# Storing the sampling hats of a deformable convolution with columns and rows apart, and loading the row hats of both halves at once

## The chip, the cores and the metric

The kernel runs on one core of one Trainium2 chip. A core has a matrix engine (PE), a vector engine (DVE), an activation engine (ACT), a general engine (POOL) and a queue processor (SP) that here only issues transfers. Each engine takes its instructions in order, and they meet through semaphores. Transfers are issued from three queues (SP, ACT and POOL) and are carried by 16 DMA engines that all queues share. The metric is the device time of one execution in microseconds (us), lower is better. Three runs of the kernel before took 9085.48, 9095.87 and 9104.18 us; the median is 9095.87 us.

## The reference

Two layers are computed on 32 images of 96 channels and 56 x 56 pixels, in float32.

The first is a squeeze-and-excite block: a 1x1 convolution to 576 hidden channels, a depthwise 3x3 convolution, a gate per channel from the mean of each hidden channel, a 1x1 convolution back to 96 channels, and the residual. Its result is called x1.

The second takes spectra of x1 by two-dimensional Fourier transforms, makes a channel gate `ca` and a pixel gate `sa` from them, and forms y = x1 * ca * sa. From y it computes 18 offsets per pixel (nine taps, two coordinates), a gate and an ordinary 3x3 convolution. Then comes the deformable convolution:

```python
px = xx + off[:, :, 0]
py = yy + off[:, :, 1]
sampled = _grid_sample_taps(y, px, py)      # bilinear: four neighbours, four weights
y_def = jnp.einsum('bcthw,oct->bohw', sampled, def_w.reshape(c, c, 9)) + def_b
z = (1 - gate) * y_base + gate * y_def
```

z is normalised over the batch, x1 is added, and a ReLU follows. Bilinear sampling at px weighs column i with max(0, 1 - |i - px|), and likewise for rows. That function is the "hat" of this text: the weight of a pixel is its column hat times its row hat.

## The kernel before

**Tiles of the sampling.** An image is cut into 7 bands of 8 rows. A band holds 14 tile columns (`NTX`) of 4 pixels, and each has two tiles of 4 x 4 pixels, an upper (s = 0) and a lower one (s = 1). A tile samples from the 8 x 8 pixels around it (`SB` = 8, `NS` = 64). For a tile the weights are a matrix of 64 source pixels by 9 taps x 16 pixels (`KP` = 144). Upper and lower tile lie on partitions 0 to 63 and 64 to 127, so that a weight tile has 128 partitions. A band is worked in two halves h of 7 tile columns (`NTH`), so that a row of a weight tile holds 7 x 144 = 1008 numbers, which is 4032 bytes.

**How the hats are made.** `offsets` (lines 651 to 688) copies the offsets of a band from PSUM (L661), stores them to DRAM as `od` (L665, POOL queue), and loads them back eight times over as `ht` (L677, SP queue): 112 partitions, one for each of 8 positions i and 14 tile columns t, and in the free dimension four pieces of 144 numbers in the order column hats of s = 0, row hats of s = 0, column hats of s = 1, row hats of s = 1. Its inner function `hats` takes |ht + blk| and then relu(1 - ...) in place (L682 and L683, both on ACT), and stores the result as `hd[x][i][t][n]` (L685, ACT queue), x being the piece of the four.

**How they are loaded.** `weights_load` (L691) fills two tiles of 128 x 1008 for one half of a band by four transfers on SP's queue. For s = 0 and for s = 1, `wc` takes column hats (L698) with the eight rows i repeated as a block, and `wr` takes row hats (L699) with each row i repeated eight times. Each transfer fills 64 partitions. The source pattern of L698 is 8 (step 0) x 8 x 1008, that of L699 is 8 x 8 (step 0) x 1008. `weights` multiplies the two tiles on DVE (L705), and the result feeds the sampling matmuls of `sample_tiles` (L734), 28 for each half. The pool of `wc` has three buffers and that of `wr` two. All pools have a buffer set for each tile name.

**What runs beside it.** While the bands of image b are sampled, image b + 1 goes through `attend` (the projection at L329 from `hq` tiles that SP loads at L311, then the Fourier transforms, whose inputs SP loads at L369 into the same `hq` tiles, the matmuls L393 and the sums L379), and image b + 2 goes through `hidden` (matmuls L169, depthwise taps on DVE at L262). `pump` steps these two streams. The half bands give a natural count: 14 of them make one image, and one image takes about 265 us. The projection begins at the start of an image's 14 half bands, and the first transform comes two half bands later.

**What sets the order.** Instructions of PE, DVE, ACT and POOL are put in order by a scheduler that works with its own estimates of durations. SP's queue is left out of that and keeps the order of the program text: a transfer that waits holds up all transfers behind it. The tile `hq` has one buffer for each of its two names.

Of the kernel before, what the change touches and what calls it, by code (L numbers as in the profile page):

```python
# [7 lines left out]
FP = mybir.dt.float32  # L8
I32 = mybir.dt.int32
AF = mybir.ActivationFunctionType  # L10
# [27 lines left out]
NTX = W // TS  # L38
NTH = NTX // 2
# [3 lines left out]
SB = TS + 2 * REACH  # L43
NS = SB * SB
KP = NTAP * TP
# [580 lines left out]
def joint_conv(nc, p, yp, j, hid):  # L626


    w = p["w"]
    pa = bank(p)  # L630
    conv3(nc, pa[:, :BW], w["joint"], yp, CJ, j)
    nc.scalar.activation(hid, pa[:DMID, :BW], AF.Relu, bias=w["dg1b"][:DMID])  # L632
    yb = p["yb"].tile([C, BW], FP, name="yb")
    yield yb, pa[OFF0 : OFF0 + NOFF, :BW]
    nc.scalar.activation(yb[BC:], pa[OFF0 + QC :, :BW], AF.Identity, bias=w["cv"]("base_b")[BC:])
    pb = bank(p)
    for k in range(NTAP):
        dy, dx = divmod(k, 3)
        r0 = j * RB + dy + PD - 1
        for i in range(2):  # L640
            nc.tensor.matmul(pb[i * BC : (i + 1) * BC, : BW // 2].rearrange("p (h w) -> p h w", h=RB // 2), w["base"][:, k],  # L641
                             yp[:C, r0 + i * RB // 2 : r0 + (i + 1) * RB // 2, dx + PD - 1 : dx + PD - 1 + W],
                             start=(k == 0), stop=(k == NTAP - 1))
    yield
    for i in range(2):
        nc.scalar.activation(yb[:BC, i * BW // 2 : (i + 1) * BW // 2], pb[i * BC : (i + 1) * BC, : BW // 2], AF.Identity,
                             bias=w["cv"]("base_b")[:BC])
    yield


def offsets(nc, p, yp, j, top, hid, ybs, hds, defer):

    w = p["w"]
    joint = joint_conv(nc, p, yp, j, hid)
    yb, pa = next(joint)
    ybs.append(yb)
    at = p["off"].tile([NOFF, NTX, 2, TP], FP, name="at")
    for s in range(2):  # L660
        nc.vector.tensor_copy(at[:, :, s].rearrange("o t (r c) -> o t r c", r=TS),  # L661
                              pa[:, s * BW // 2 : (s + 1) * BW // 2].rearrange("o (r t c) -> o t r c", r=TS, t=NTX))
    yield
    od = p["dp"].tile([NTX, 2, NOFF, TP], FP, name="od")
    nc.gpsimd.dma_start(od.rearrange("t s o p -> o (t s) p"), at.rearrange("o t s p -> o (t s) p"))  # L665
    yield
    next(joint)
    yield
    next(joint)
    yield  # L670
    next(joint, None)
    nc.vector.tensor_reduce(top, at.rearrange("o t s p -> o (t s p)"), AX.X, ALU.max, apply_absolute_value=True)
    for _ in range(4):
        yield
    ht = p["ht"].tile([SB * NTX, 4, KP], FP, name="ht")
    src = od.rearrange("t s o p -> t (s o p)").unsqueeze(0).to_broadcast([SB, NTX, 4 * KP])
    nc.sync.dma_start(ht.rearrange("q n k -> q (n k)"), src)  # L677
    for _ in range(6):
        yield

    def hats():
        p["tc"].keep_in_program_order(nc.scalar.activation(ht, ht, AF.Abs, bias=w["blk"]))  # L682
        nc.scalar.activation(ht, ht, AF.Relu, bias=w["one"], scale=-1.0)  # L683
        hd = p["dp"].tile([4, SB, NTX, KP], FP, name="hd")
        nc.scalar.dma_start(hd.rearrange("x i t n -> (i t) x n"), ht)  # L685
        hds.append(hd)

    defer(hats)


def weights_load(nc, p, hd, h):  # L691

    src = hd.rearrange("n i t k -> n i (t k)")[:, :, h * NTH * KP : (h + 1) * NTH * KP]
    wc = p["wc"].tile([2 * NS, NTH * KP], FP, name="wc")
    wr = p["wr"].tile([2 * NS, NTH * KP], FP, name="wr")
    for s in range(2):
        ps = slice(s * NS, (s + 1) * NS)
        nc.sync.dma_start(wc[ps], src[2 * s].unsqueeze(0).to_broadcast([SB, SB, NTH * KP]))  # L698
        nc.sync.dma_start(wr[ps], src[2 * s + 1].unsqueeze(1).to_broadcast([SB, SB, NTH * KP]))  # L699
    return wc, wr  # L700


# [246 lines left out]
def layers(tc, a, dp, x1d, zd, stats, far):  # L949
# [8 lines left out]
    with ExitStack() as ctx:  # L958
# [144 lines left out]
        def prepare(upto):  # L1103

            nonlocal n_loads
            while n_loads < min(upto, 2 * len(hds)):
                n, m = divmod(n_loads, 2)
                loads.append(weights_load(nc, p, hds[n], m))
                n_loads += 1
# [402 lines left out]
```

## Time and profile before

| | before |
|---|---|
| median of three runs | 9095.87 us |
| profiled execution | 9085.91 us |
| its span, first to last instruction | 9084.1 us |
| PE busy | 8142.0 us (90%) |
| DVE busy | 7141.8 us (79%) |
| ACT busy | 5374.6 us (59%) |
| POOL busy | 2782.8 us (31%) |
| granted PE clock, mean | 0.943 |
| DMA moved | 1486.53 MB, 164 GB/s |
| `wc` transfers (L698) | 896 of 252 KB |
| `wr` transfers (L699) | 896 of 252 KB |

The profile is of one execution, so a sum made on it is made against 9085.91 us, which lies 9.96 us under the median. In the span's 40 slices PE is busy nine tenths or more from the fourth to the thirty-seventh. The end is different: from 8800 to 9084 us PE does nothing, and the normalisation moves data at 407 GB/s. In a view of waits a line names the instruction that waited, its engine, and what released it, then the total in us, the number of waits and the longest. In a view of windows the columns are the stretch, its length, the busy time of five engines with their counts of instructions, the granted clock (1.00 is full), the mean busy share of the 16 DMA engines, and GB/s.

### The profile page before, as it was taken

The page shows a single profiled execution, that of the slowest core. Times are in us where ns is not written, and L with a number is a line of the kernel's source. Part 1 is how long each engine was busy: PE and PEld are TensorE (multiplying, and loading weights), DVE is VectorE, ACT ScalarE, POOL GpSimd, SP SyncE. Part 2 cuts the span into 40 slices and gives each one's busy share as a digit, 9 for nine tenths or more (in the row PEclk, how much of TensorE's full clock was granted, in tenths as well). Part 3 has the DMA queues.
Part 4 walks back from the last instruction along what each step waited for, and adds up shares of the span by engine and source line. Part 5 has one row for each costly group of instructions (what it writes and reads, how often), then busy time and mean ns, then how long its engine had stood idle before and what let it go on. Part 6 is the DMA issues. An engine that isn't in the chain of part 4 may idle for free. (4 is left out here: it accounts for less than half of the span.)

```text
span 9084.1 us, 138191 instructions
## 1 busy us (share of the span) xinstructions
PE 8142.0 (90%) x52406; PEld 5146.5 (57%) x52406; DVE 7141.8 (79%) x6821; ACT 5374.6 (59%) x10486; POOL 2782.8 (31%) x2608
## 2 busy tenths in 40 slices
PE   5889999999999999999999999999999999999860
PEld 3455565565555566555655655565565555566640
DVE  7688788888878788888888888788888888887333
ACT  2356666666656566666666666665666666666553
POOL 0123233333323333332333333233333323333210
PEclk9889999999999999999999999999999999999985
DMA  2355555555555555555555555555655555555559
GB/s 84 104 142 164 162 167 163 165 152 153 166 163 167 163 166 152 154 163 164 167 165 163 156 153 163 162 168 164 166 153 152 165 163 164 167 166 146 127 183 417
DMA packets 1068763, 1486.53 MB, mean 164 GB/s; under 512 B 590190, under 2 KB 839838, under 8 KB 1055806
## 3 DMA queue, kind: packets, MB, share of 16 engines
q1 hardware_dynamic: 858995, 985.20, 39.8%
q10 hardware_dynamic: 153803, 329.80, 10.0%
q0 software_dynamic: 55296, 162.60, 7.0%
q8 instruction: 421, 6.90, 0.3%
q14 instruction: 248, 2.03, 0.1%
HBM read 1064.29 MB, written 412.65 MB: 163 GB/s over the span
## 5 line engine op out<-in xcount | busy, mean ns | idle before, releaser
L262 DVE SCALAR_TENSOR_TENSOR acch<-hp,w,acch 128x1512 f32<-128x1512 f32 (+1 forms) x2250 | 4344.6, 1931 | 34.9
L716 POOL COPY ybl<-yp 96x448 f32<-96x448 f32 x896 | 1247.4, 1419 | 1671.1 <-PE mm L720 1670.2
L612 PE MATMUL mm<-yp,c_jointW 104*128 104x448 f32 x4032 | 1713.0, 577 | 37.4 <-DMA yp<-fqd 37.3
L753 PE MATMUL pd<-v,c_def 128*96 128x224 f32 (+1 forms) x6272 | 1371.4, 364 | 39.9 <-ACT v L738 38.3
L612 PEld LDWEIGHTS mm<-yp,c_jointW 104*128 104x128 f32 x4032 | 790.9, 200 | 846.7 <-issue 798.8
L753 PEld LDWEIGHTS pd<-v,c_def 128*96 128x96 f32 (+1 forms) x6272 | 1002.8, 166 | 317.4 <-issue 95.6
L173 ACT ACTIVATE hp<-mm,sh,inv 128x392 f32<-128x392 f32 (+2 forms) x1216 | 812.9, 673 | 572.7 <-PE mm L169 483.2
L169 PE MATMUL mm<-xt,w 96*128 96x392 f32 (+3 forms) x2688 | 1074.1, 540 | 37.2 <-DMA xt<-in_x 33.2
L738 ACT COPY v<-mm 96x288 f32<-96x288 f32 (+1 forms) x2688 | 1005.1, 443 | 103.7 <-PE mm L734 65.4
L734 PE MATMUL mm<-wc,yt 64*96 64x144 f32 x12544 | 1031.0, 295 | 15.2 <-issue 6.0
L705 DVE TENSOR_TENSOR wc<-wc,wr 128x1008 f32<-128x1008 f32 x448 | 573.6, 1280 | 548.9 <-DMA wr<-hd 437.2
L734 PEld LDWEIGHTS mm<-wc,yt 64*96 64x96 f32 x12544 | 812.3, 160 | 302.0 <-issue 186.6
L329 PE MATMUL mm<-hq,w3s 128*96 128x392 f32 x2048 | 797.5, 536 | 149.9 <-DMA hq<-h2d 148.4
L665 POOL DMA_DIRECT2D od<-at x224 | 186.2, 831 | 2112.9 <-DVE at L661 1487.8
L641 PE MATMUL mm<-yp,c_base0W 96*64 96x224 f32 x8064 | 827.0, 357 | 0.0
L745 ACT COPY v<-v 32x448 f32<-32x448 f32 x1344 | 755.2, 562 | 30.3
L641 PEld LDWEIGHTS mm<-yp,c_base0W 96*64 96x64 f32 x8064 | 552.8, 135 | 276.2 <-issue 70.4
L722 ACT COPY yt<-mm 128x384 f32<-128x384 f32 (+1 forms) x896 | 350.6, 440 | 529.2 <-PE mm L720 517.7
L222 ACT ACTIVATE acch<-acch,sh,inv 128x1568 f32<-128x1568 f32 x288 | 488.7, 1697 | 259.2 <-DVE acch L262 256.7
L632 ACT ACTIVATE hid<-mm,c_dg1b 50x448 f32<-50x448 f32 x224 | 140.7, 628 | 838.5 <-PE mm L612 806.7
L329 PEld LDWEIGHTS mm<-hq,w3s 128*96 128x96 f32 x2048 | 339.7, 175 | 505.3 <-issue 472.5
L473 POOL TENSOR_TENSOR o<-o,xc 96x392 f32<-96x392 f32 x256 | 369.8, 1445 | 671.4 <-ACT o L339 670.0
(194 smaller groups left out, 9104.2 us busy)
## 6 DMA issues: line engine op xcount, KB each, us to landing
h2d<-acch ACTq DMA_DIRECT2D x288, 784.0 KB
wc<-hd SPq DMA_DIRECT2D x896, 252.0 KB
wr<-hd SPq DMA_DIRECT2D x896, 252.0 KB
hq<-h2d SPq DMA_DIRECT2D x128, 980.0 KB
hq<-h2d SPq DMA_DIRECT2D x128, 784.0 KB
hq<-x1d SPq DMA_DIRECT2D x768, 98.0 KB
ht<-od SPq DMA_DIRECT2D x224, 252.0 KB
hd<-ht ACTq DMA_DIRECT2D x224, 252.0 KB
```

The lines of the kernel that those rows point to most:

```text
L169: nc.tensor.matmul(pt[p0 : p0 + w1.shape[1], : rows * W], w1, xts[hf][:, r0 * W : (r0 + rows) * W], start=True, stop=True)
L173: nc.scalar.activation(h1[lo:hi, row0 : row0 + rows, 1 : 1 + W], pt[lo:hi, : rows * W].rearrange("p (h w) -> p h w", h=rows), AF.Silu, bia ...
L262: nc.vector.scalar_tensor_tensor(acc[:, lo:hi], win, wk, acc[:, lo:hi], ALU.mult, ALU.add)
L329: nc.tensor.matmul(pts[half][:C, :EW], w3s[:, ch], hq, start=(i == 0), stop=False)
L612: nc.tensor.matmul(view, weights[:, k], yp[:channels, r0 : r0 + RB, dx + PD - 1 : dx + PD - 1 + W], start=(k == 0), stop=(k == NTAP - 1))
L641: nc.tensor.matmul(pb[i * BC : (i + 1) * BC, : BW // 2].rearrange("p (h w) -> p h w", h=RB // 2), w["base"][:, k], yp[:C, r0 + i * RB // 2 ...
L705: p["tc"].keep_in_program_order(nc.vector.tensor_tensor(wc, wc, wr, ALU.mult))
L716: nc.gpsimd.tensor_copy(yb[:, :, s], blocks)
L734: nc.tensor.matmul(pt[k][:C, (t - lo) * KP : (t - lo + 1) * KP], yt[ps, t], s[ps, t * KP : (t + 1) * KP], start=True, stop=True)
L738: nc.scalar.copy(v[:C, :, lo:hi, k].rearrange("c k t p -> c t k p"), pt[k][:C, : (hi - lo) * KP].rearrange("c (t k p) -> c t k p", t=hi - ...
L745: nc.scalar.copy(v[C:, 1 + 2 * i : 3 + 2 * i], v[i * QC : (i + 1) * QC, KA:])
L753: nc.tensor.matmul(out.rearrange("c q (t x) -> c t q x", x=TS), p["w"]["def"][ks, k], v[ks, k].rearrange("c t s (r x) -> c t (s r) x", r=T ...
```

## The change

The hats are written to a second tile `ho` with the two s of the column hats side by side, followed by the two s of the row hats, and `hd` gets the matching shape [2, 2, i, t, n]. The first activation writes this order, the second works in place on `ho`. In `weights_load` the two `wr` transfers become one whose source is 16 x 8 (step 0) x 1008 and which fills all 128 partitions. The two `wc` transfers keep their shape (8 (step 0) x 8 x 1008, 64 partitions each) and now stand in front of the `wr` transfer.

```diff
     def hats():
-        p["tc"].keep_in_program_order(nc.scalar.activation(ht, ht, AF.Abs, bias=w["blk"]))
-        nc.scalar.activation(ht, ht, AF.Relu, bias=w["one"], scale=-1.0)
-        hd = p["dp"].tile([4, SB, NTX, KP], FP, name="hd")
-        nc.scalar.dma_start(hd.rearrange("x i t n -> (i t) x n"), ht)
+        ho = p["ht"].tile([SB * NTX, 2, 2, KP], FP, name="ho")
+        p["tc"].keep_in_program_order(nc.scalar.activation(
+            ho.rearrange("q x s n -> q s x n"), ht.rearrange("q (s x) n -> q s x n", s=2), AF.Abs, bias=w["blk"]))
+        nc.scalar.activation(ho, ho, AF.Relu, bias=w["one"], scale=-1.0)
+        hd = p["dp"].tile([2, 2, SB, NTX, KP], FP, name="hd")
+        nc.scalar.dma_start(hd.rearrange("x s i t n -> (i t) (x s) n"), ho.rearrange("q x s n -> q (x s) n"))
         hds.append(hd)
...
 def weights_load(nc, p, hd, h):
-    src = hd.rearrange("n i t k -> n i (t k)")[:, :, h * NTH * KP : (h + 1) * NTH * KP]
+    cols, rows = (hd[x].rearrange("s i t k -> (s i) (t k)")[:, h * NTH * KP : (h + 1) * NTH * KP] for x in range(2))
     wc = p["wc"].tile([2 * NS, NTH * KP], FP, name="wc")
     wr = p["wr"].tile([2 * NS, NTH * KP], FP, name="wr")
     for s in range(2):
-        ps = slice(s * NS, (s + 1) * NS)
-        nc.sync.dma_start(wc[ps], src[2 * s].unsqueeze(0).to_broadcast([SB, SB, NTH * KP]))
-        nc.sync.dma_start(wr[ps], src[2 * s + 1].unsqueeze(1).to_broadcast([SB, SB, NTH * KP]))
+        nc.sync.dma_start(wc[s * NS : (s + 1) * NS], cols[s * SB : (s + 1) * SB].unsqueeze(0).to_broadcast([SB, SB, NTH * KP]))
+    nc.sync.dma_start(wr, rows.unsqueeze(1).to_broadcast([2 * SB, SB, NTH * KP]))
     return wc, wr
```

In the built programs SP's queue shrinks from 3638 to 3190 instructions, all else of it in the same order. The scheduler's order moves a little on the other engines: PE has the same 28468 instructions, with 244 places that hold another one than before. On DVE the product L705 stands one to four instructions earlier in 134 of its 448 places, in most of them ahead of one tap of L262.

## The prediction

> **What bounds the kernel now.** I read the page first, then the waits of PE, then the waits of SP and DVE, then the order of time around one of PE's stalls, and last some windows for the load on the DMA engines.
>
> From the page: PE is the busiest engine, and it is fed from its own order.
>
> ```profile
> PE 8142.0 (90%) x52406; PEld 5146.5 (57%) x52406; DVE 7141.8 (79%) x6821; ACT 5374.6 (59%) x10486; POOL 2782.8 (31%) x2608
> PEclk9889999999999999999999999999999999999985
> ```
>
> The tail without PE (284 us) and the start are untouched by this change. Between 430 and 8400 us PE is busy 94% of the time. What can be won there is a stall of PE, so its waits come next, longest first:
>
> ```profile
> PE mm L329 <- DMA hq<-h2d: 148.4, 31, 7.7
> PE mm L393 <- DVE sq L379: 89.0, 23, 5.2
> PE acc L437 <- DVE m_fe L434: 59.1, 31, 2.0
> PE mm L720 <- POOL ybl L716: 50.1, 30, 2.0
> ...
> PE mm L393 <- DMA hq<-x1d: 39.3, 9, 10.2
> ...
> PE mm L734 <- DVE wc L705: 4.5, 1, 4.5
> ```
>
> The reader should see two things. The weight tiles of this change hold PE directly for 4.5 us only, so a sum over their own consumer gives next to nothing. But the two longest waits, once per image each, are for things that come through the same DMA queue: L329 waits 148.4 us for `hq`, L393 waits 89.0 + 39.3 = 128.3 us, partly for `hq` and partly for the sums L379 on DVE.
>
> DVE's longest wait is for the row hats:
>
> ```profile
> DVE wc L705 <- DMA wr<-hd: 437.2, 122, 16.6
> ```
>
> The order of time in image 15 shows how that reaches PE. SP first, then DVE, then PE, from the timelines of 4479 to 4500 us (start, length, line):
>
> ```profile
> 4479.82 2.84 SPq L369 DMA_DIRECT2D hq<-x1d  x6
> 4482.71 0.59 SPq L698 DMA_DIRECT2D wc<-hd  x1
> 4483.41 1.15 SPq L699 DMA_DIRECT2D wr<-hd  x1
> 4484.60 2.20 SPq L698 DMA_DIRECT2D wc<-hd  x1
> 4486.85 0.57 SPq L699 DMA_DIRECT2D wr<-hd  x1
> 4487.54 0.66 SPq L677 DMA_DIRECT2D ht<-od  x1
> 4488.30 7.48 SPq L369 DMA_DIRECT2D hq<-x1d  x6
> ...
> 4494.20 1.21 DVE L705 TENSOR_TENSOR wc<-wc,wr 128x1008 f32<-128x1008 f32 x1 [7.99 <-DMA wr<-hd]
> 4495.33 1.15 DVE L379 TENSOR_REDUCE sq<-mm 112x56 f32<-112x448 f32 x2
> ...
> 4496.39 2.03 PE L393 MATMUL mm<-c_FU,hq 112*128 112x116 f32 x8 [2.47 <-DMA hq<-x1d]
> ```
>
> The weight loads are issued by 4487.4 and land near 4494. The six `hq` loads behind them are issued in 7.48 us where six took 2.84 us before, so the queue was backed up. L379 stands behind the product on DVE, and PE waits for both.
>
> Last, windows that tell how wide these transfers are. From 7960 to 7964 us only weight loads move (the packets in flight are all of their size), and from 8900 to 8910 us the wide transfers of the end:
>
> ```profile
> 7960.00:7964.00 4.00, 4.00 (x29) 2.88 (x29) 3.44 (x4) 2.38 (x5) 0.00 (x0) 1.00 0.50 137
> 8900.00:8910.00 10.00, 0.00 (x0) 0.00 (x0) 2.93 (x3) 3.35 (x4) 0.00 (x0) 0.50 1.01 424
> 4803.00:4812.00 9.00, 8.00 (x14) 3.79 (x15) 9.00 (x9) 5.73 (x10) 0.00 (x0) 0.62 0.22 89
> ```
>
> A queue of weight loads keeps half of the DMA engines busy (0.50) at 137 GB/s, while the end uses all (1.01). The third line is for the clock, below.
>
> **The change part by part.**
>
> *The row load on twice the engines.* One half band loads 4 x 252 KB = 1.032 MB. At 137 GB/s that is 7.5 us on eight engines. Afterwards the row half of the bytes (0.516 MB) is spread over 16, if its first dimension decides, so each of those eight carries three quarters of what it did: 5.6 us. All that is queued behind on them comes 1.9 us earlier. Bounds: nothing if the load stays on eight, 3.7 us if all four loads' share fell to half.
>
> The page "DMA: Bandwidth & Descriptors" of the Trainium skill, section "Why a DMA increments its semaphore by 16 and not by 1", says a transfer uses the largest number up to 16 that divides the slowest dimension of both its patterns. The 0.50 agrees for a pattern that begins with 8; that one beginning with 16 uses all is not shown by any run yet.
>
> *At L329.* In image 15 the first `hq` load is out at 4435.66, four weight loads follow to 4438.66, and the next `hq` loads stand behind them; PE then waits 3.34 us. Taking 1.9 us from each of 31 waits (mean 148.4 / 31 = 4.8 us) gives 59 us. Low bound 0, if the store of `h2d` that SP waits for (440.7 us in 33 waits) decides alone; high bound 148.4.
>
> *At L393.* 32 waits (23 + 9), mean 4.0 us, 1.9 us each: 61 us. Against it stands one move in the built order: in 15 images one L260 (1032 ns) is put ahead of the two L379 that PE waits for: 15 us back. Net 46 us; bounds 0 and 128.3.
>
> *One issue less.* 448 issues of 577 ns are 258 us of SP's time. SP spends far more than that waiting (1268.0 us at L698 for `hd` alone), and where it is the late one (the 2.20 us issue above) it is backed up, which is counted already. I take 0. If that cover were gone, each of the 448 loads would let the transfers behind it go 0.58 us sooner, 258 us at the very most.
>
> *The first activation.* It does the same 576 numbers in four runs of 144. The nearest rows are the in-place L683 at 774 ns and L738, which copies 432 strided numbers in 516 ns and 288 in 407. These last two give a fixed part of some 190 ns; four separate pieces would cost 3 x 190 x 224 = 128 us of ACT, none would cost 0. L738 itself is no dearer for its strides, so I take 0. ACT is 59% busy and hides either; only where ACT's hats hold a weight load of PE (16.2 us at L641) would it show. Behind L682 and L683 in ACT's queue stand the L738 copies that PE's banks need.
>
> *New waits.* L682 now waits for the store from `ho` one band before, some 38 us earlier (265 / 7). That store has long landed. `ht` comes free earlier, after L682, but L677 waited for that only once (25.1 us). Both 0. The row load waits for both buffers' halves at once, as its consumer did. The two `wc` loads move ahead of one `wr`; nothing reads a half alone.
>
> *DVE.* 122 waits shrink by 1.9 us, 232 us of idle time less at most. But 134 products stand ahead of one tap (1931 ns) or more, so there the gain is spent on standing earlier. DVE is 79% busy and does not bind; 0 beyond the L379 above.
>
> *The order on PE.* 244 places of 28468 change, mostly a block moved past one matmul (362 ns). 0, with 30 us either way as bound: 31 images times about three moved blocks of 0.3 us.
>
> *The clock.* L329 has a mean of 536 ns where its median is 492: 2048 x 44 ns = 90 us; L393 295 against 275: 61 us. So 151 us go to slow clock after these stalls. The third window above follows a stall of only 2.0 us at L437, and its granted clock is 0.62. The stalls that I leave are 2.9 and 2.1 us, so I expect the slow stretches to stay: 0, high bound 151.
>
> The page "TensorE: Matmul & The Clock Gate" (section "What's actually happening") says that the clock falls after an idle window of about 3.4 us. By that rule the remaining stalls keep full speed and the sum would be 105 + 151 = 256 us. The row with 2.0 us speaks against it, and the measurement decides.
>
> *Sum.* 59 + 46 = 105 us. The profiled execution of 9085.9 would become 8981; the median lies 10 us above it, so the prediction is 9095.9 - 105, about 8990 us.
>
> **The rivals.**
>
> *It is hidden (same).* PE's stalls belong to the store of `h2d` and to the `x1d` loads themselves, or the wide load stays on eight engines, so the change does not do what it says and only an issue goes. For it: SP waits 440.7 us for `h2d<-acch`, and PE almost never waits on L705. Against it: the 7.48 us backup behind the weight loads. Time: 9080 to 9096.
>
> *The clock comes with it (faster still).* The stalls fall under what lowers the clock: 105 + 151 us, 8840. For it: 4455 to 4506 us has two slow stretches right after the two stalls. Against it: the 2.0 us row.
>
> *The products stand too early (slower).* On DVE 134 products now stand ahead of a tap of 1.93 us. This decides once a load lands less than 1.93 us earlier than before: then DVE idles up to 134 x 1.93 = 259 us more in front of the product, and what PE needs from DVE (the sums, L434, the copies L661) comes later. PE's waits for DVE are 89 + 59 + 39 us now. If a third of it reached PE, 86 us: 9182. For it: my own 1.9 us is right at that point. Against it: in half band 2, where DVE waits longest, the product is not moved, and DVE has a fifth of its time free.
>
> **How the numbers follow.** A measurement of this kernel can tell about 0.2% (18 us) from no change. The forecast has 0.55 with a range of its own from 8900 (both places at the most that one wait allows, some clock) to 9060 (one place alone). The clock rival has 0.15, hidden 0.14, too early 0.16. Faster is thus 0.70, same 0.14, slower 0.16. For 8 in 10 the range runs from 8880, which leaves out the deep half of the clock rival, to 9110, which takes in hidden and the mild half of the slower one.
>
> **What would show it.** Right: windows with weight loads alone at a DMA share above 0.50; the L369 group behind them issued in clearly less than 7.48 us; L329's wait for `hq` near 90 us and L393's near 80; L705's wait for `wr` well under 437; L682 still near 767 ns; SP with 448 issues fewer. Wrong: the wait at L329 unchanged (the store decides), a longer wait at L705 or at L792 and L661 on DVE, or L682 near 1.3 us.

## The result, and the profile after

The changed kernel takes 9197.99 us (median of 4 runs, 9179.94 to 9207.46), beside 9096.89 us for the kernel before on the same chip: a ratio of 1.0103 with a 95% interval of 1.0089 to 1.0117. It is slower by one per cent, where the prediction had 8990 us. The profiled execution took 9207.46 us, the longest of the four, with a span of 9205.7.

The page of the changed kernel begins with the busy times. Behind line 688 its lines are one higher than before (L705 is now L706, L734 is L735, L753 is L754); L682, L683 and L685 are L683, L685 and L687.

```profile
span 9205.7 us, 137176 instructions
PE 8268.1 (90%) x52406; PEld 5227.4 (57%) x52406; DVE 7205.9 (78%) x6821; ACT 5382.4 (58%) x10486; POOL 2692.7 (29%) x2608
```

The span grew by 121.6 us, and PE's busy time by 126.1 us (8142.0 before) with the same 52406 records. What PE did not do, span less busy, is 942.1 us before and 937.6 us after. So PE does not stand still for longer: the same matmuls take longer. The granted clock says so as well, 0.930 in the mean where it was 0.943.

The waits of PE, longest first (the line that waited, what released it, total us, number, longest):

```profile
PE mm L393 <- DVE sq L379: 124.7, 29, 5.9
PE mm L329 <- DMA hq<-h2d: 94.8, 31, 5.8
PE mm L735 <- ACT yb L646: 67.6, 28, 2.8
PE acc L437 <- DVE m_fe L434: 58.1, 30, 2.1
PE mm L735 <- ACT hp L173: 42.9, 31, 1.6
```

The wait at L329 fell by 53.6 us, nearly the 59 of the prediction. The wait at L720 for `ybl` (50.1 us before) is gone from this list. In its place stand two waits of the sampling matmuls, L735, for ACT's copies at L646 and L173: 110.5 us, 28 and 31 times in 32 images. The next fence has what waits on DVE and on SP's queue.

```profile
DVE wc L706 <- DMA wr<-hd: 511.3, 126, 16.0
DVE z L793 <- PE pd L754: 235.8, 96, 11.4
DVE yp L599 <- DMA yp<-x1d: 204.1, 72, 9.3
...
SPq L677 <- DMA od<-at: 1048.6, 108, 20.4
```

These were 437.2, 123.1, 74.6 and 571.1 us. DVE waits longer for the row hats than before, though they come by the wider load. This wait alone says little of the time: `layout_only` below, with narrow loads and the old order, has 493.5 us of it and takes no longer than before.

Last, a window in which hardly anything but weight loads moves (columns as before: length, busy time of five engines, granted clock, mean busy share of the 16 DMA engines, GB/s).

```profile
8449.00:8456.00 7.00, 7.00 (x81) 4.71 (x78) 6.99 (x8) 1.09 (x3) 0.00 (x0) 1.00 0.76 129
```

Before, such a window had a share of 0.50 at 137 GB/s. The load now does occupy more of the engines, but alone it moves no more bytes in a microsecond. For loads that are nearly alone in the trace, the time from the first packet of the four or three transfers to the last is 8.11 us before and 7.91 after (medians of 56 and 116 loads), and a packet of 4032 bytes takes 244 ns before and 359 after in the mean. Loads that run beside other transfers are another matter, and the experiments come back to them. The page's line on the queue says the same for the whole run: 985.20 MB both times, 39.8% of the engines' time before and 45.9% after.

### The profile page after: what moved, and what is told of

Same layout as the page of the kernel before. It is cut to its first block, busy times and chain, and to the rows that moved or that the text cites. A ratio compares the mean times of both kernels' runs of the same rounds, so it can differ in the third digit from the quotient of the medians.

```text
span 9205.7 us, 137176 instructions
## 1 busy us (share of the span) xinstructions
PE 8268.1 (90%) x52406; PEld 5227.4 (57%) x52406; DVE 7205.9 (78%) x6821; ACT 5382.4 (58%) x10486; POOL 2692.7 (29%) x2608
## 3 DMA queue, kind: packets, MB, share of 16 engines
q1 hardware_dynamic: 858995, 985.20, 45.9%
## 5 line engine op out<-in xcount | busy, mean ns | idle before, releaser
L262 DVE SCALAR_TENSOR_TENSOR acch<-hp,w,acch 128x1512 f32<-128x1512 f32 (+1 forms) x2250 | 4369.2, 1942 | 37.0
L612 PE MATMUL mm<-yp,c_jointW 104*128 104x448 f32 x4032 | 1710.1, 577 | 2.5 <-ACT yt L723 1.5
L717 POOL COPY ybl<-yp 96x448 f32<-96x448 f32 x896 | 1085.0, 1239 | 1703.7 <-PE mm L721 1703.7
L754 PE MATMUL pd<-v,c_def 128*96 128x224 f32 (+1 forms) x6272 | 1420.1, 373 | 15.5 <-ACT v L739 13.9
L612 PEld LDWEIGHTS mm<-yp,c_jointW 104*128 104x128 f32 x4032 | 791.7, 200 | 806.1 <-issue 752.6
L754 PEld LDWEIGHTS pd<-v,c_def 128*96 128x96 f32 (+1 forms) x6272 | 1032.7, 171 | 317.4 <-issue 100.0
L735 PE MATMUL mm<-wc,yt 64*96 64x144 f32 x12544 | 1092.9, 302 | 126.0 <-ACT yb L646 67.6
L173 ACT ACTIVATE hp<-mm,sh,inv 128x392 f32<-128x392 f32 (+2 forms) x1216 | 812.8, 673 | 509.9 <-PE mm L169 426.5
L735 PEld LDWEIGHTS mm<-wc,yt 64*96 64x96 f32 x12544 | 852.0, 165 | 440.0 <-issue 192.1
L706 DVE TENSOR_TENSOR wc<-wc,wr 128x1008 f32<-128x1008 f32 x448 | 567.0, 1266 | 521.2 <-DMA wr<-hd 511.3
L329 PE MATMUL mm<-hq,w3s 128*96 128x392 f32 x2048 | 783.3, 528 | 96.3 <-DMA hq<-h2d 94.8
L641 PE MATMUL mm<-yp,c_base0W 96*64 96x224 f32 x8064 | 827.5, 357 | 0.0
L641 PEld LDWEIGHTS mm<-yp,c_base0W 96*64 96x64 f32 x8064 | 553.3, 135 | 276.3 <-issue 69.9
L473 POOL TENSOR_TENSOR o<-o,xc 96x392 f32<-96x392 f32 x256 | 400.4, 1564 | 674.1 <-ACT o L339 672.6
L393 PE MATMUL mm<-c_FU,hq 112*128 112x116 f32 x3072 | 451.2, 294 | 152.2 <-DVE sq L379 124.7
```

The costliest lines, as they stand in the source:

```text
L173: nc.scalar.activation(h1[lo:hi, row0 : row0 + rows, 1 : 1 + W], pt[lo:hi, : rows * W].rearrange("p (h w) -> p h w", h=rows), AF.Silu, bia ...
L262: nc.vector.scalar_tensor_tensor(acc[:, lo:hi], win, wk, acc[:, lo:hi], ALU.mult, ALU.add)
L329: nc.tensor.matmul(pts[half][:C, :EW], w3s[:, ch], hq, start=(i == 0), stop=False)
L612: nc.tensor.matmul(view, weights[:, k], yp[:channels, r0 : r0 + RB, dx + PD - 1 : dx + PD - 1 + W], start=(k == 0), stop=(k == NTAP - 1))
L706: p["tc"].keep_in_program_order(nc.vector.tensor_tensor(wc, wc, wr, ALU.mult))
L717: nc.gpsimd.tensor_copy(yb[:, :, s], blocks)
```

## The experiments

The change alters two things at once: what is loaded, and, through the scheduler's estimates, the order of instructions on PE, DVE, ACT and POOL. The first runs take these apart. All ratios are against the kernel before on the same chip.

**Loads and order apart.** To write an order out, an edge without a wait goes from every instruction of an engine to the one before it in a list taken from the other built program. That adds no instruction.

```diff
-        nc.vector.tensor_scalar(far, every, (SB - 1) / 2, None, ALU.is_gt)
+        nc.vector.tensor_scalar(far, every, (SB - 1) / 2, None, ALU.is_gt); pin_order(tc)
...
+        for k in range(1, n):
+            a, b = mine[int(order[k - 1])], mine[int(order[k])]
+            tc.add_manual_dep(b, a.name, mybir.DependencyInfo(mybir.DependencyClass.NoSync, mybir.DependencyReason.DATA),
+                              reason="pin_order")
```

`wide_oldorder` is the changed kernel with the order of before on the four engines:

> The changed kernel (new hats, one row load of 16 x 8 x 1008), but with the instructions of PE, DVE, ACT and POOL held in the order of the kernel before. Theory A, the moved order costs the time and the wide load itself is good: L329's wait near 95 us as in the changed kernel, no stall of the sampling matmuls on L646 and L173, and a time under that of before, about 9000 to 9060 us. Theory B, the wide load itself costs it, since a weight load of 1.03 MB alone took 8.1 us before and still takes about 7.9 us while its packets keep 16 engines busy instead of 8: a time near that of the changed kernel, 9150 to 9200 us.

`narrow_neworder` is the kernel before with the order of the changed one:

> The kernel before (old hats, four loads on eight engines), but with the instructions of PE, DVE, ACT and POOL held in the order that the changed kernel has. Theory A, the order costs the time: about 9200 us, with new waits of the sampling matmuls on L646 and L173 in every image. Theory B, the wide load costs it: about 9097 us, within 18 us.

`layout_only` has the new hats and four narrow loads. The scheduler gives it the order of before by itself:

```diff
     for s in range(2):
         nc.sync.dma_start(wc[s * NS : (s + 1) * NS], cols[s * SB : (s + 1) * SB].unsqueeze(0).to_broadcast([SB, SB, NTH * KP]))
-    nc.sync.dma_start(wr, rows.unsqueeze(1).to_broadcast([2 * SB, SB, NTH * KP]))
+        nc.sync.dma_start(wr[s * NS : (s + 1) * NS], rows[s * SB : (s + 1) * SB].unsqueeze(1).to_broadcast([SB, SB, NTH * KP]))
```

> The new order of the hats in SBUF and DRAM and the second tile, but four loads of 64 partitions as before; the instruction order on all engines comes out as that of the kernel before. Theories A and B both expect the time of before, 9097 us within 18 us, L682's successor near 767 ns. A third theory, that the strided activation or the new tile costs the time, expects 9190 us and an activation well over 800 ns.

Measured: `wide_oldorder` 9024.21 us, ratio 0.9916 [0.9898, 0.9935]; `narrow_neworder` 9245.77 us, 1.0151 [1.0125, 1.0176]; `layout_only` 9098.64 us, 1.0 [0.9989, 1.001].

So the layout costs nothing, the wide load alone is worth 0.84%, and the order loses 1.5% with narrow loads and 1.9% with wide ones (1.0103 / 0.9916). `wide_oldorder` beats both kernels. Of its waits of PE:

```profile
PE mm L329 <- DMA hq<-h2d: 93.8, 31, 4.2
PE mm L393 <- DVE sq L379: 87.5, 22, 6.2
PE mm L721 <- POOL ybl L717: 64.8, 29, 3.7
...
PE mm L393 <- DMA hq<-x1d: 39.6, 9, 10.3
```

The reader sees the gain at L329 (148.4 before), no gain at L393 (127.1 us in both lines, 128.3 before), and L721 still waiting for `ybl`. With narrow loads in the new order it is the other way round: the two new waits are there, and L329 is where it was.

```profile
PE mm L329 <- DMA hq<-h2d: 147.0, 31, 7.6
PE mm L734 <- ACT yb L646: 68.0, 28, 2.8
...
PE mm L734 <- ACT hp L173: 42.9, 31, 1.6
```

**Why a load alone hardly drains faster.** `wide_distinct` has the order of the changed kernel, and its row load reads 128 different rows of the input instead of 16 rows eight times each:

```diff
-    nc.sync.dma_start(wr, rows.unsqueeze(1).to_broadcast([2 * SB, SB, NTH * KP]))
+    nc.sync.dma_start(wr, p["plain"].rearrange("c h w -> (c h w)")[: 2 * NS * NTH * KP].rearrange("(q n) -> q n", n=NTH * KP))
```

> The changed kernel in its own instruction order, but the row load reads 128 different rows of 4032 bytes from the input image in place of 16 rows that are each read eight times; the row hats are left out of the product in this way. If the reading of the same rows again and again is what keeps the load at 128 GB/s: the packets get shorter, the SP queue's share of the DMA engines falls from 45.9% to under 40%, and DVE's wait for the row load falls well under 511 us. If the engines or the SBUF side limit it: share and wait as in the changed kernel.

`narrow_distinct`, in the same order, takes the rows by two loads of 64 partitions whose source begins with eight, out of different rows too (both kernels leave the row hats out of the product, so only their times count):

```diff
+        nc.sync.dma_start(wr[s * NS : (s + 1) * NS], p["plain"].rearrange("c h w -> (c h w)")[s * 64640 : (s + 1) * 64640].rearrange("(q z) -> q z", z=8080)[:, :8064].rearrange("q (r n) -> q r n", n=NTH * KP))
```

> Order of the changed kernel on all engines; the row weights come by two loads of 64 partitions that begin with a dimension of eight, out of 64 different rows each of the input x, so the row hats are left out of the product. With one load of 128 different rows it was 0.9956 of before (load alone 6.55 us, against 7.91 with each row read eight times over sixteen engines). Theory, different rows are what helps, whatever the width: 0.993 to 1.000, and a load alone takes 6.4 to 6.8 us. Rival, it needs the sixteen engines as well: 1.008 to 1.016, as with narrow loads in this order (1.0151), and a load alone takes 7.5 to 8.1 us.

Measured: `wide_distinct` 9062.2 us, 0.9956 [0.994, 0.9972], a load alone in 6.55 us; `narrow_distinct` 9231.87 us, 1.0159 [1.0137, 1.018], a load alone in 8.18 us. The windows with weight loads nearly alone, first of `wide_distinct`:

```profile
8490.00:8495.50 5.50, 5.50 (x48) 3.93 (x47) 2.33 (x4) 2.24 (x5) 0.82 (x1) 1.00 0.81 174
```

and of `narrow_distinct`:

```profile
8449.00:8456.00 7.00, 7.00 (x56) 5.18 (x53) 6.12 (x7) 1.41 (x3) 0.00 (x0) 1.00 0.50 135
```

Different rows alone change nothing (0.50 of the engines at 135 GB/s, as before the change). A load that is alone gains from the width only where its rows differ: 174 GB/s against 129. The rival of that run holds. With the same sixteen rows read eight times over, twice the engines move the same bytes in the same time. What in the memory limits that was not taken apart.

**What the wide load gains at L329.** The load that PE waits behind at L329 is not alone. The packets in the traces give, for the last weight load ahead of each wait of PE over 1 us, the time from its first packet to its last (means; the last line counts only loads beside which other transfers moved less than 25 GB/s):

| weight loads, us | before | `wide_oldorder` | changed kernel |
|---|---|---|---|
| ahead of 30 waits at L329 | 11.28 | 8.23 | 8.32 |
| ahead of 32 waits at L393 | 7.81 | 7.70 | 8.12 |
| nearly alone | 8.17 | 7.86 | 7.93 |

At L329 the transfers beside the load moved 1.98 MB before, at L393 0.41 MB. At L329, in this crowd, the load lands 3 us sooner with its rows on sixteen engines, and from its first packet to the matmul that waited it takes 14.06 us instead of 15.89. It is the width that does it: with narrow loads in the new order the same load takes 11.11 us, with narrow loads of different rows 11.20, with the wide load of different rows 8.03. The issue that the wide load saves takes 0.58 us, so it can be the smaller part of the 1.8 us at most.

**Which engine's order.** Six more kernels with the wide load, each engine in the old or in the new order. First PE alone in the new order, then PE alone in the old, then DVE alone in the new:

> The changed kernel's loads, PE in the new order, DVE, ACT and POOL in the old one. With all engines in the old order this code took 0.9916 of before, with all in the new order 1.0103, so 1.9% (about 170 us) belong to the order. Theory A, the one matmul per image that PE now does behind the next band's block: nearly all comes back, 1.006 to 1.011 (9150 to 9200 us), PE's wait for the sums of the blend on DVE near 236 us as in the changed kernel. Theory B, DVE's products, copies and sums moved against each other: this kernel stays at 0.990 to 0.995 (9010 to 9050 us). Theory C, both needed together: about 0.999 to 1.002.

> The complement: PE in the old order, DVE, ACT and POOL in the new one, loads of the changed kernel. Theory A (PE's matmul): 0.990 to 0.995, 9010 to 9050 us. Theory B (the other engines' order): 1.006 to 1.011, 9150 to 9200 us, with PE's new waits for yb and hp still there. Theory C: about 0.999 to 1.002.

> Only DVE in the new order, PE, ACT and POOL in the old one, loads of the changed kernel. If DVE's order costs by itself: 1.004 or more. If it costs nothing: 0.990 to 0.995 as with all engines in the old order. Beside the run with ACT and POOL in the new order too it tells their share.

The first expectation rests on the largest move that I found on PE. Once per image the last of seven matmuls L753 that finish a tile `pd` stands behind the next band's convolutions (nine of L612, eighteen of L641, some 10 us) instead of ahead of them, and the blend on DVE (L792) waits for `pd`. It fell, as the table shows, and the next ones were made for POOL:

> Loads of the changed kernel; DVE and POOL in the new order, PE and ACT in the old. With DVE alone new it was 0.9993, with DVE, POOL and ACT new 1.0114. Theory, POOL's copies and stores in the new order let PE run some 5 us ahead in half band 9, where it then waits for the band's copies on ACT: 1.009 to 1.013, with PE's two waits for yb and hp there, about 70 and 42 us. Rival, it is ACT's order: 0.997 to 1.002 without those waits.

> Loads of the changed kernel; POOL alone in the new order, the others in the old. If POOL's order is enough for the two waits of PE: 1.008 or more. If it takes DVE's new order as well: 0.989 to 0.997, as with all in the old order.

> The changed kernel with POOL alone put back to the old order. If POOL's order is what the changed kernel loses by: 0.992 to 1.002. If the new order of PE and DVE costs as much against the old one of POOL (as PE alone new did, 1.0157): 1.008 to 1.02, and then it is the fit of the four orders and no single one that counts.

| kernel (wide load) | PE | DVE | ACT | POOL | us | ratio, interval | PE busy, us | span less busy, us |
|---|---|---|---|---|---|---|---|---|
| `wide_oldorder` | old | old | old | old | 9024.21 | 0.9916 [0.9898, 0.9935] | 8137.9 | 878.9 |
| `wide_dvenew` | old | new | old | old | 9090.98 | 0.9993 [0.998, 1.0007] | 8151.5 | 937.8 |
| `wide_poolnew` | old | old | old | new | 9111.34 | 1.001 [0.9998, 1.0023] | 8230.3 | 880.3 |
| `wide_dvepool` | old | new | old | new | 9200.15 | 1.0105 [1.008, 1.013] | 8246.3 | 946.0 |
| `wide_peold` | old | new | new | new | 9193.09 | 1.0114 [1.0095, 1.0132] | 8254.4 | 930.9 |
| changed kernel | new | new | new | new | 9197.99 | 1.0103 [1.0089, 1.0117] | 8268.1 | 937.6 |
| `after_poolold` | new | new | new | old | 9094.78 | 0.9991 [0.9977, 1.0004] | 8157.7 | 931.0 |
| `wide_penew` | new | old | old | old | 9238.09 | 1.0157 [1.0138, 1.0177] | 8249.0 | 1006.7 |

Two engines carry the loss. DVE's order costs 0.8% (0.9916 to 0.9993), most of it as standing time of PE: 59 us of 72.5 us of span. POOL's costs 0.9% from the old order, 1.1% beside DVE's new one, and 1.1% when it alone is put back in the changed kernel, nearly all of it as longer matmuls: 92 us of busy time in 94 us of span. Both together give the time of the changed kernel, and ACT's and PE's new orders add nothing to it. The matmul that I suspected costs 2.4% when PE alone has it. DVE then still asks for `pd` early, as this wait of DVE in `wide_penew` shows (185.1 us in `wide_oldorder`):

```profile
DVE z L793 <- PE pd L754: 358.7, 83, 15.5
```

In the changed kernel DVE's own order has moved with it. One order can't be judged without the others.

**What DVE's order does.** Where DVE alone is new, these are the two waits of PE that grew most; in `wide_oldorder` the first is 87.5 us and the second is not among the longest:

```profile
PE mm L393 <- DVE sq L379: 107.0, 27, 6.3
...
PE mm L777 <- DVE sq L379: 37.2, 13, 5.4
```

DVE's wait for the row hats at L706 is 526.8 us there, and 395.9 us in `wide_oldorder`. The products stand earlier, wait 131 us more for loads that are not there yet, and the sums behind them come later. PE's two waits grew by 19.5 and 37.2 us, of which 16.3 us come off again at L393's wait for `hq` (39.6 to 23.3). That the moved products cause this is read from the waits, and L706's own is a weak witness (it moved by 56 us between the kernel before and `layout_only`, at no cost); the single moves of DVE's order were not tried apart.

**What POOL's order does.** The timeline of POOL in image 10 of `wide_oldorder`, up to the copies for half band 9 (start, length, line):

```profile
3255.70 0.85 POOL L665 DMA_DIRECT2D od<-at  x1
3256.57 1.23 POOL L373 TENSOR_TENSOR hq<-hq,sa 112x448 f32<-112x448 f32 x1
3257.75 6.31 POOL L717 COPY ybl<-yp 96x448 f32<-96x448 f32 x2
```

PE waits for the second of these copies:

```profile
3264.12 0.80 PE L721 MATMUL mm<-c_ident,ybl 96*128 96x96 f32 x7 [1.82 <-POOL ybl L717]
```

The same place in `wide_poolnew`. The product L373 has gone ahead of the store and of the copies:

```profile
3281.47 5.27 POOL L373 TENSOR_TENSOR hq<-hq,sa 112x448 f32<-112x448 f32 x2
3286.70 1.06 POOL L593 DMA_DIRECT2D sab<-sad  x2
3287.75 0.85 POOL L665 DMA_DIRECT2D od<-at  x1
3288.60 1.07 POOL L717 COPY ybl<-yp 96x448 f32<-96x448 f32 x2
```

The copies take 1.07 us instead of 6.31 (what lengthened them was not tried), and PE no longer waits there. It runs ahead, and stands some 30 us later. The PE timeline of `wide_poolnew`, then ACT's:

```profile
3321.76 0.48 PE L735 MATMUL mm<-wc,yt 64*96 64x144 f32 x2 [2.78 <-ACT yb L646]
3323.75 1.27 PE L735 MATMUL mm<-wc,yt 64*96 64x144 f32 x6 [1.51 <-ACT hp L173]
```

```profile
3316.54 0.63 ACT L635 ACTIVATE yb<-mm,c_cvec 32x448 f32<-32x448 f32 x1 [6.81 <-DVE at L661]
```

L646 stands behind L635 in ACT's queue, and L635 waits 6.81 us for DVE's copy L661. DVE is not early, so a PE that is early gains nothing: its wait of 1.82 us is traded for 4.29 us in two pieces. What follows them is the larger part. Sixteen microseconds from the same point of the half band (some 4 us behind the start of its product L706), first of `wide_oldorder`, then of `wide_poolnew`:

```profile
3284.00:3300.00 16.00, 16.00 (x149) 11.99 (x140) 12.28 (x12) 14.56 (x26) 4.29 (x6) 1.00 0.56 121
```

```profile
3316.00:3332.00 16.00, 11.51 (x61) 8.06 (x60) 12.74 (x14) 14.71 (x26) 3.29 (x5) 0.71 0.65 142
```

In the one the granted clock is 1.00 and PE busy throughout, in the other it is 0.71. Summed over the run, PE's standing time is the same in the two kernels (878.9 and 880.3 us), and longer matmuls carry the 92 us. The records of the granted clock agree: each slow stretch times what it lacks to full clock sums to 493 us over `wide_oldorder` and to 598 over `wide_poolnew`, and half band 9 goes from 0.2 to 4.8 us an image. The groups of PE in `wide_oldorder` (busy us, mean ns, idle before):

```profile
L754 PE MATMUL pd<-v,c_def 128*96 128x224 f32 (+1 forms) x6272 | 1369.8, 363 | 43.9 <-ACT v L739 42.1 <-ACT v L746 1.1 <-DVE z L793 0.7
...
L735 PE MATMUL mm<-wc,yt 64*96 64x144 f32 x12544 | 1039.0, 297 | 13.8 <-DVE wc L706 7.2 <-ACT hp L173 2.5 <-ACT v L746 2.5
```

and in `wide_poolnew`:

```profile
L754 PE MATMUL pd<-v,c_def 128*96 128x224 f32 (+1 forms) x6272 | 1404.2, 370 | 17.1 <-ACT v L739 15.9 <-ACT v L746 1.1
L735 PE MATMUL mm<-wc,yt 64*96 64x144 f32 x12544 | 1092.0, 303 | 127.4 <-ACT yb L646 70.1 <-ACT hp L173 44.1 <-DVE wc L706 7.6
```

L735 is 53 us longer and L754 34 us. The changed kernel has the same place in nearly every image, with 2.78 and 1.51 us in image 10 and a clock of 0.70 from 3341 to 3357 us.

**Is it the stall or the clock?** If the pair of stalls brings on the slow clock, work that fills the first of them should give time back. `after_filled` issues the seven transposes ahead of it four times, `after_filled2` the four sampling matmuls ahead of it three times:

```diff
-        for t in range(lo, hi):
+        for t in (*range(lo, hi),) * (1 + EXTRA * (n in FILL)):
             nc.tensor.transpose(pt[:, (t - lo) * C : (t - lo + 1) * C], yb[:, t].rearrange("c s r x -> c (s r x)"),
...
-        for t in range(lo, hi):
+        for t in (*range(lo, hi),) * (1 + EXTRA * (n in FILL and lo == group[0][0])):
             for k in range(2):
```

> The changed kernel with its own order, and one addition: in half band 9 of each image the seven transposes of the sampled blocks are issued four times instead of once into the same bank (same result), 21 more matmuls per image, by some 107 ns each 2.25 us, just ahead of the pair of stalls of PE at the sampling matmuls (2.78 and 1.2 to 1.5 us). Theory, the pair of stalls costs mostly by the slow clock that follows it (4.88 us per image in this half band): the first stall shrinks to some 0.5 us, the work added fits in it, the clock lost there falls to 0 to 2 us per image, and 90 to 150 us come back: 0.994 to 1.001 of before (9050 to 9105 us). Rival, the time belongs to the chain on DVE and ACT that PE waits for, and the clock only shows the waiting: 1.009 to 1.014, no gain.

> The changed kernel with its own order, and one addition: in half band 9 of each image the four sampling matmuls just ahead of the pair of stalls of PE are issued three times instead of once into the same banks (same result), 8 more instructions per image, some 2.4 us of true matmuls where the run before had 2.25 us of transposes. Theory, the pair of stalls costs by the slow clock that it brings on, and transposes did not keep the clock up: the clock lost in this half band falls from 4.88 us per image to under 2, and the time to 0.995 to 1.003 of before. Rival, the time is set by what PE waits for there: 1.008 to 1.014, whatever the clock does.

Measured: 9189.63 us, 1.01 [1.0083, 1.0117], and 9203.99 us, 1.0119 [1.0099, 1.0138]; the changed kernel has 1.0103. Neither gave time back. The same sum over the records of the clock, as a mean over 29 images, gives for half band 9 4.88 us in the changed kernel, 3.71 with the transposes and 4.18 with the matmuls, while the stalls of L735 there went from 108 us to 75 and 81 us in the whole run (the first of the pair from 2.4 us in the mean to 1.4 and 1.5). The slow stretch stayed with the second stall, which neither run touches. So the loss is measured as slow clock, but what sets it off there is not settled: to shorten the first stall was not enough. The profiled execution of `after_filled` was at 9146.85 us the fastest of its five and is not typical of it.

## Why the prediction was wrong

**The row load on twice the engines: right in a crowd, not alone.** The prediction let all that is queued behind the load come 1.9 us earlier wherever PE waits, since each engine carries three quarters of the bytes. The share did rise, from 0.50 to 0.76. But it took an engine's rate as fixed, and for a load alone a packet went from 244 to 359 ns and the load ends 0.2 us sooner (8.11 to 7.91): there its low bound, nothing, was the nearer one. Among the other transfers at L329 the load ends 3 us sooner. The Trainium skill's page "DMA: Bandwidth & Descriptors", in the section that the prediction cites, gives the count of engines rightly for this pattern; it does not say what the engines then move, and here that was 129 GB/s after 137 for a load alone.

**At L329: right.** 54.6 us in `wide_oldorder`, 53.6 us in the changed kernel, predicted 59, or 1.8 us a wait against 1.9. That the figure fits so well is in part luck: it was worked out from the rate of a load alone, and such a load gains nearly nothing.

**At L393: a term that was mis-sized.** Predicted 61 us, less 15 for a move of DVE's order. With the old order, where that move is absent, 1.2 us came (128.3 to 127.1), and in the changed kernel 16 us were lost (124.7 + 19.7 = 144.4). The loads ahead of these waits run nearly alone and take 7.7 us as before (7.81 to 7.70). The six `hq` loads behind one of them in image 15 are issued in 9.12 us in `wide_oldorder`, where the prediction looked for clearly less than 7.48.

**The first activation and the new waits: right, nothing.** `layout_only` has the activations and the store of the change at a ratio of 1.0. The one issue less was not tried alone, so its 0 is not shown.

**DVE, "0 beyond the L379 above": a step that failed.** It cost 0.77% at equal loads (0.9916 to 0.9993), some 70 us. The rival "the products stand too early" has the mechanism: it said that this decides once a load lands less than 1.93 us earlier, that DVE would idle up to 259 us more ahead of the product, and that a third of it would reach PE. The mean of all loads is 0.8 us shorter (8.85 us before, 8.06 in `wide_dvenew`), DVE idled 131 us more, and 59 us reached PE. Its 9182 us lies near the measured 9198 by luck, for it has no term for POOL, and DVE's new order alone ends at 9090.98. Against it the prediction put that DVE has a fifth of its time free; as the waits read, that did not protect PE, because the sums that PE waits for stand behind the products in the queue.

**The order on PE, "0, with 30 us either way": right for this kernel, and read wrongly.** I took it for a block moved past one matmul. It is a matmul moved behind a block, and alone it costs 2.4% (0.9916 to 1.0157). It costs nothing here because DVE's order moved with it.

**POOL's order: a step that is missing.** The working has SP, ACT, DVE and PE and no term for the order of POOL, where 49 blocks of instructions change places. They are the larger part of the loss: 1.1%, some 102 us, come back when POOL alone has the old order (1.0103 to 0.9991).

**The clock, "0, high bound 151": wrong in sign.** I only asked whether stalls would go, not whether new ones could come. PE's busy time grew by 126 us, and what the slow stretches lack to full clock went from 514 to 642 us. The page "TensorE: Matmul & The Clock Gate" (section "What's actually happening") has the clock fall after an idle window of about 3.4 us. Here it fell at 3322.85 us of `wide_poolnew`, within the second of two stalls of 2.78 and 1.51 us that lie 0.48 us apart. Neither is as long as that window, though together they leave PE idle for 4.29 of 4.77 us. The 2.0 us row in the prediction had shown a fall with a single stall already.

**The sum.** From before to `wide_oldorder` the profiled spans fall by 67.3 us, where the prediction has 59 + 61 = 120 before the 15 us that it takes off for DVE's order: the mechanism, an earlier `hq` at L329, was right, and L393 was not. What turned a gain into a loss is the order: no term for POOL, and 0 for DVE and for the clock. From there DVE's order adds 72.5 us of span and POOL's another 103.0 (`wide_dvepool`, 9192.3), and the changed kernel ends at 9205.7.

## What to carry to other kernels

An edit to one transfer can move every engine's order where a scheduler works with estimates. Compare the two orders engine by engine, the idle ones too, and pin the old order to see what the edit itself is worth: here the edit gained 0.8% and its new order lost 1.9%. An engine that is let go earlier gains nothing if what it meets next is paced by another; look for the wait that it runs into. Measure a load at the waits that it is meant to shorten: alone, more DMA engines hardly hastened this one, because its packets took longer, and among other transfers they took 3 us off it.

## What the runs showed of the hardware that I had not expected

A weight load alone, whose row transfer reads each of sixteen DRAM rows eight times over, moved 129 GB/s with that transfer on sixteen engines where it had moved 137 GB/s on eight; with 128 different rows it moved 174 GB/s. On eight engines it made no difference whether the rows repeat (137 and 135 GB/s). Beside some 1.5 to 2 MB of other transfers the same load took 11.3 us on eight engines and 8.2 us with its rows on sixteen.

PE's standing time stayed the same to 2 us in 880 while its busy time grew by 92 us: its stalls moved to a place behind which the granted clock fell. In the changed kernel a stall of about 2 us at L437 was followed by no slow clock in 10 of 28 images and by a slow stretch in the other 18, so the length of a stall alone doesn't tell.
